# Four chained image layers: u's last steps before z's last product, zero products at the start, and a written order for the last half

## The chip, the cores and the metric

The kernel runs on one core of one Trainium2 chip. The metric is the device time of one execution in microseconds. Besides, one execution was taken with the hardware profiler, and every line of a profile below comes from that execution.

## The reference

The input x has 8 images of 512 channels and 32 x 32 = 1024 pixels, in float32. Four layers follow one another, each on the whole of the one before:

```python
# layer 0: products of two normed projections, scaled by their largest singular value
f, g = relu(batchnorm(Wf @ x)), relu(batchnorm(Wg @ x));  h = Wh @ x      # 64 x 1024 per image
z = f.T @ g;  x = Wv @ (z / sigma_max(z) @ h.T).T + x
# layer 1: group norm, attention of 1024 pixels over 512 channels
n = group_norm(x);  x = x + Wp @ (softmax(q(n).T @ k(n) / sqrt(512)) @ v(n))
# layer 2: attention with 128 channels, then a projection z back to 512
x = bn(Z @ (softmax(t.T @ p / sqrt(128)) @ g)) + x
# layer 3: binary 512 x 512 product
y = (sign(W) * mean|W|) @ sign(x + bias);  t = bn(y) + x - shift
out = where(t > 0, t, slope * t) + bias2
```

The change touches the places where layer 2 ends and layer 3 begins for each image, where layer 1 of the next image starts, the very start, and the very end.

## The kernel before, in words

**Stages.** In the first some 180 us all images go through layer 0's projections (loop over `b`, `products` at L1380 to L1389: 64 x 512 products of weights `fg` and `h` with x). For image 0 the loop runs over the four blocks `cc` of 128 channels and does both f and g for a block before it takes the next. The x tile of an image is loaded by `load_x` (L136) on SP's queue, one transfer per channel block, the first block of image 0 in two halves; the weights `fg` come over ScalarE's queue, one transfer per block. After the statistics, singular values and folded weights are made, `fast` (L919) is called for one image after another, eight times. In it TensorE's program is the order in which the Python text draws it (`manual_schedule` for PE); the order of the other engines' instructions is set by a planner, which goes by its own estimate of when each is ready. An instruction marked with `keep_in_program_order` stays where the text has it. On every engine the instructions then run in that fixed order.

**Two-by-two products with seven multiplications.** Large products are cut into 2 x 2 blocks and done with seven block products, `seven` (L350). Its steps are, in order: A11B11, S1T1, S2T2, S4B22, S3T3, A12B21, A22T4. Each is drawn by one `next`. S1T1, S2T2 and so on are products of sums of blocks. A11B11, S2T2, S3T3 and A22T4 accumulate in one PSUM bank, S1T1 and S4B22 in another; after each step the bank is read by ScalarE (`move`, L358 or L360) or added to the result by VectorE (`plus`, L364 or L366). So A22T4 may only start when the addition after S3T3 has read the bank. The matmuls of all these products have line L413. One product of 128 x 128 weights by 512 pixels in float32 shows as two records 0.43 us apart.

**u.** `make_u` (L498) makes u = wu n for the *next* image, in two groups of seven steps. Behind the last step VectorE makes the block sums of u (`sums_of`, L326): S1 (L331), S2 (L334), S3 in place (L335) and S4 (L336), which the scores of the next image need. The steps are a generator, `steps`, and `fill(k)` draws k of them, as work with which TensorE covers waits.

**The end of layer 2 and layer 3.** `close2` (L705) multiplies z's weights by the attention result of one half (512 pixels): four products (L709), each added to x by VectorE (L711). `leave` (L713) is layer 3 for a half: ScalarE takes the signs of the four channel blocks (L720), TensorE multiplies them by the packed signs of the weights in float16 (L732), ScalarE and VectorE unpack (L743 to L745), scale and add x (L753), and form the two-sided slope: relu (L775), scale (L776), sum (L783), store (L787). For the images with a successor the second half of `leave` stops after the signs, is put into `rest3`, and is taken up by the next call of `fast`: after the first and after the third step of its scores (`scores1`) one `next` is drawn, and each begins with a sign product.

The order of the text before, per image with a successor, is then: the first half of layer 3; `close2` of the second half; the signs of the second half; two more steps of u by `fill(2)`; the rest of u; the next image's scores.

**The last image.** Its layer 3 uses unpacked signs, one product per 128 output channels (L732, `signs`). The first half and the first pair of products of the second take VectorE's maximum (L759), ScalarE's scale (L762) and GpSimd's sum (L769); the last pair goes by relu, scale and VectorE's sum (L775, L776, L783), the very last in two halves of 256. `count_bad` (L801) counts values out of bounds with one small product (L823), casts it (L824) and loads the number into a register of every engine (L825), since a branch (L1778) at the end decides on it whether a slower path runs. In the order of the text this load stands behind the first product of the second half.

Of the kernel before, what the change touches and what calls it, by code (L numbers as in the profile page):

```python
# [16 lines left out]
P = 128  # L17
# [70 lines left out]
def kernel(  # L88
# [55 lines left out]
    def half(i):  # L144
        return bass.ts(i, HF)
# [8 lines left out]
    def load_w(name, src, shape, pool=wpool, eng=nc.sync, tag=None):  # L154
        t = pool.tile(shape, F32, tag=tag or name, name=name)
        eng.dma_start(out=t, in_=src)
        sbw[name] = t
        return t
# [6 lines left out]
    for cc in range(CC):  # L165
        nc.scalar.dma_start(out=fg[:, cc, :], in_=w_fg[:, cc, :])
    first = load_x(0, True)
    load_w("h", w_h, [P, CC, MID], a1, nc.scalar)


# [64 lines left out]
    def col(name, i):  # L235
        return ct[:, COL[name] + i : COL[name] + i + 1]
# [476 lines left out]
    def leave(env, xt, dst, halves=range(NH), signs=None, stop=False):  # L713


        small = env["small"]
        for h in halves:
            sg = env["e"].tile([P, CC, HF], F16, tag="e", name="sg")
            for cc in range(CC):
                nc.scalar.activation(  # L720
                    sg[:, cc, :], xt[:, cc, half(h)], AF.Sign, bias=rb3[:, cc : cc + 1]
                )
            if stop:
                yield
            for j in range(CC // 2):
                both = env["e"].tile([P, 2, HF], F32, tag="e", name="both")
                y1, y2 = both[:, 0, :], both[:, 1, :]

                def product(lt):
                    ps = bank()  # L730
                    for cc in range(CC):
                        mm(  # L732
                            out=ps,
                            lhsT=lt[:, cc, bass.ts(j, P)],
                            rhs=sg[:, cc, :],
                            start=cc == 0,
                            stop=cc == CC - 1,
                        )
                    return ps

                if signs is None:
                    ps = product(sw3)
                    nc.scalar.activation(y2, ps, AF.Identity, bias=round3, scale=1.0 / PACK)  # L743
                    nc.vector.tensor_scalar(y2, y2, ROUND, None, ALU.subtract)
                    nc.vector.scalar_tensor_tensor(y1, y2, -PACK, ps, ALU.mult, ALU.add)  # L745
                    sums = y1, y2
                else:
                    sums = [product(signs[0])]
                    yield
                    sums.append(product(signs[1]))  # L750

                for y, ps, oc in ((y1, sums[0], j), (y2, sums[1], j + 2)):
                    nc.vector.scalar_tensor_tensor(  # L753
                        y, ps, sa3[:, oc : oc + 1], xt[:, oc, half(h)], ALU.mult, ALU.add
                    )
                    up = small.tile([P, HF], F32, tag="half_a", name="up3")
                    if signs is not None and (h == 0 or j == 0):

                        nc.vector.tensor_scalar(  # L759
                            up, y, nc3[:, oc : oc + 1], ps3[:, oc : oc + 1], ALU.max, ALU.mult  # L760
                        )
                        nc.scalar.activation(  # L762
                            y,
                            y,
                            AF.Identity,
                            bias=qb3[:, oc : oc + 1],
                            scale=col("L3_conv_pr_slope", oc),
                        )
                        nc.gpsimd.tensor_tensor(y, y, up, ALU.add)  # L769
                        nc.sync.dma_start(out=dst[:, oc, half(h)], in_=y)  # L770
                        continue
                    final = signs is not None and y is y2
                    for q in (slice(0, HF // 2), slice(HF // 2, HF)) if final else [slice(0, HF)]:
                        yq, uq = y[:, q], up[:, q]
                        nc.scalar.activation(uq, yq, AF.Relu, bias=cb3[:, oc : oc + 1])  # L775
                        nc.scalar.activation(  # L776
                            yq,
                            yq,
                            AF.Identity,
                            bias=pb3[:, oc : oc + 1],  # L780
                            scale=col("L3_conv_pr_slope", oc),
                        )
                        nc.vector.scalar_tensor_tensor(  # L783
                            yq, uq, ps3[:, oc : oc + 1], yq, ALU.mult, ALU.add
                        )
                        to = slice(h * HF + q.start, h * HF + q.stop)
                        nc.sync.dma_start(out=dst[:, oc, to], in_=yq)  # L787
                yield

    def unpacked(env):  # L790

# [127 lines left out]
    def fast(env, n, hb, ua):  # L919
# [90 lines left out]
        if more:  # L1010
            r = inverse_sums(env, esum, B + n)
            values2(0, range(2, NTH))
            att = values2(0, range(NTH, NT))
            values2(1, range(0, NTH))
            close2(xt, att, 0)
            att = values2(1, range(NTH, NT))
            fill()
            for i, _ in enumerate(leave(env, xt, dst, [0])):
                fill(2 * (i % 2))
            close2(xt, att, 1)  # L1020
            rest3.append(leave(env, xt, dst, [1], stop=True))
            next(rest3[0])
            fill(2)
            for _ in steps:
                pass
        else:


            r = inverse_rows(env, esum, B + n)
            att = values2(0, range(2, NT))  # L1030
            values2(1, range(0, 2))
            close2(xt, att, 0)
            values2(1, range(2, 6))
            before, after = leave(env, xt, dst, [0], signs), leave(env, xt, dst, [1], signs)
            count = count_bad(env)
            next(count)
            next(before)
            next(before)
            att = values2(1, range(6, NT))
            next(before)  # L1040
            close2(xt, att, 1)
            for _ in before:
                pass
            next(after)
            next(count)
            for _ in after:
                pass
# [322 lines left out]
    for b in range(B):  # L1370
        xt = load_x(b) if b else first
        for name, src, pool in later.get(b, ()):
            load_w(name, src, shapes.get(name, [P, CC, C]), pool)
        if b in (2, 3, 4, 5):
            load_blocks(*((("q", w_q), ("k", w_k))[b // 2 - 1]), ((0, 1), (2, 3))[b % 2])
        if b >= B - 2:
            resident[b] = xt
        banks = [bank() for _ in w0[: 3 if b < B - 2 else 2]]

        def products(i, cc):  # L1380
            for h in range(NH):
                mm(
                    out=banks[i][side(h), :],
                    lhsT=w0[i][:, cc, :],
                    rhs=xt[:, cc, half(h)],
                    start=cc == 0,
                    stop=cc == CC - 1,
                )

        if b == 0:  # L1390
            for cc in range(CC):
                for i in range(2):
                    products(i, cc)
        for i in range(3):
            if i == 2 and b >= B - 2:
                continue
            if b or i == 2:
                for cc in range(CC):
                    products(i, cc)
            if i == 0:  # L1400
                nc.scalar.copy(fs[b], banks[i])
                nc.vector.bn_stats(st[:, 0, b, :], fs[b])
            elif i == 1:
                nc.vector.tensor_copy(gs[b], banks[i])
                nc.vector.bn_stats(st[:, 1, b, :], gs[b])
                if last is not None:
                    turn(last[0], last[1], ht_pair[last[0] // 2], 0)
        if b < B - 2:
            hraw = a2.tile([P, HF], F32, tag="hraw", name="hraw")
            nc.scalar.activation(hraw, banks[2], AF.Identity, bias=bhc)  # L1410
            last = b, hraw
        else:
            last = None
        if b == 3:
            total3 = sign_weights()
        if b == 5:
            scale_signs(total3)
        if b > 5:
            natural(*((("q", "w3"), ("k", "q"))[b - 6]))
# [415 lines left out]
```

## Time and profile before

| | us |
|---|---|
| median of 3 runs (1883.66 to 1883.94) | 1883.89 |
| the profiled execution | 1883.68 |
| its span, first to last instruction | 1881.8 |
| TensorE busy in the span | 1854.7 |
| VectorE, ScalarE, GpSimd busy | 1124.5, 540.8, 121.8 |
| mean granted TensorE clock | 0.998 |

The profile's page gives busy times, the costliest groups of instructions and the chain that ended last; further views list who waited for whom, and the instructions of one engine in order of time. In a line of the timeline the first number is the start in us from the beginning of the span, the second the time from there to the end of the last of the instructions merged in the line; then come the engine, the line in the code, the operation, `output<-inputs`, and at the end how many. In brackets stands how long the engine had been idle, and who released it. Letters: PE is TensorE's matmul, PEld its weight load, DVE VectorE, ACT ScalarE, POOL GpSimd, SP the queue of most transfers. In a list of waits the numbers are the total in us, how often, and the longest. Names of tiles: `bank` is a PSUM bank, `ut` is u, `us` its block sums, `h` and `hs` the normed image and its block sums, `wu` and `su` the weights of u and their sums, `att` the attention result, `z` z's weights, `xt` the image, `sg` its signs, `sw` and `signs` the packed and unpacked signs of layer 3's weights, `both` and `up` the working tiles of layer 3.

### The profile page before, as it was taken

Reading aid. Unit: us, or ns where it says so; the run is one execution under the profiler, and the core shown is the slowest. Engines: PE = TensorE matmul, PEld = TensorE weight load, DVE = VectorE, ACT = ScalarE, POOL = GpSimd, SP = SyncE. Lnnn points to the kernel's source line nnn. Section 1 sums busy time; section 2 is a strip of 40 time slices with the busy share of each in tenths; the row PEclk is TensorE's granted clock in tenths of the full one; section 3 lists DMA queues with packets and bytes.
Section 4 is the critical chain, followed back from the end, with each engine's and each line's share of the span. In section 5 each row is a group of like instructions: output and inputs, shape, how many; then the busy total and the mean of one; then the engine's idle time right before and its main releaser. Section 6 shows DMA issues by size and latency. Waiting matters only on the chain. (4 is left out here: it accounts for less than half of the span.)

```text
span 1881.8 us, 16542 instructions
## 1 busy us (share of the span) xinstructions
PE 1854.7 (99%) x6196; PEld 948.8 (50%) x6196; DVE 1124.5 (60%) x2083; ACT 540.8 (29%) x882; POOL 121.8 (6%) x109
## 2 busy tenths in 40 slices
PE   8999999999999999999999999999999999999997
PEld 4365464544644464544645465544644464544653
DVE  3356777466744767566754676356633766355447
ACT  2042220343113521244202521244203521243113
POOL 1000002000010001100020001100110001000011
PEclk9999999999999999999999999999999999999999
DMA  8620000002000200002000200002000200000001
GB/s 280 200 85 7 1 17 1 1 34 73 12 1 12 90 17 1 1 34 73 12 1 12 90 18 0 1 34 67 12 0 12 90 12 0 1 34 23 12 0 47
DMA packets 32738, 66.52 MB, mean 35 GB/s; under 512 B 4944, under 2 KB 12300, under 8 KB 32524
## 3 DMA queue, kind: packets, MB, share of 16 engines
q1 hardware_dynamic: 31724, 64.96, 10.4%
q8 instruction: 51, 0.84, 0.2%
q10 hardware_dynamic: 864, 0.43, 0.1%
q14 instruction: 35, 0.29, 0.1%
q0 software_dynamic: 64, 0.00, 0.0%
HBM read 46.44 MB, written 18.94 MB: 35 GB/s over the span
## 5 line engine op out<-in xcount | busy, mean ns | idle before, releaser
L591 PE MATMUL bank<-e,vt 128*128 128x512 f32 x768 | 336.2, 594 | 0.0
L591 PEld LDWEIGHTS bank<-e,vt 128*128 128x128 f32 x768 | 144.3, 190 | 172.3 <-issue 167.9
L413 PE MATMUL bank<-ut,h 128*128 128x512 f32 x384 | 178.5, 599 | 0.2
L413 PEld LDWEIGHTS bank<-ut,h 128*128 128x128 f32 x384 | 70.7, 190 | 97.4 <-issue 91.3
L413 PE MATMUL bank<-us,hs 128*128 128x512 f32 x256 | 115.6, 593 | 0.0
L840 PE MATMUL bank<-tpg 128*128 128x512 f32 x256 | 115.4, 595 | 0.0
L993 PE MATMUL bank<-e,tpg 128*128 128x512 f32 x256 | 114.7, 595 | 0.0
L364 DVE TENSOR_TENSOR e<-bank,e 128x512 f32<-128x512 f32 x96 | 66.2, 689 | 62.9 <-PE bank L413 57.5
L847 ACT ACTIVATE e<-bank 128x512 f32<-128x512 f32 x128 | 76.3, 597 | 67.0 <-PE bank L840 67.0
L358 ACT COPY e<-bank 128x512 f32<-128x512 f32 x96 | 56.0, 583 | 123.4 <-PE bank L413 123.4
L413 PE MATMUL bank<-wo,h 128*128 128x256 f32 x384 | 89.8, 384 | 0.0
L413 PE MATMUL bank<-h,wu 128*128 128x512 f32 x192 | 89.0, 594 | 0.8 <-DVE h L488 0.8
L244 POOL TENSOR_TENSOR r_r<-r_v,minus_half 128x4 f32<-128x4 f32 (+1 forms) x11 | 10.8, 987 | 1050.5 <-DVE r_v L243 1045.2
L993 PEld LDWEIGHTS bank<-e,tpg 128*128 128x128 f32 x256 | 48.1, 190 | 60.4 <-issue 60.0
L413 PEld LDWEIGHTS bank<-wo,h 128*128 128x128 f32 x384 | 71.4, 190 | 12.6 <-issue 3.8
L413 PEld LDWEIGHTS bank<-us,hs 128*128 128x128 f32 x256 | 48.4, 190 | 57.5 <-issue 56.2
L852 DVE TENSOR_TENSOR esum<-esum,e 128x1024 f32<-128x1024 f32 x48 | 58.8, 1226 | 30.1 <-ACT e L847 29.9
L840 PEld LDWEIGHTS bank<-tpg 128*128 128x128 f32 x256 | 47.6, 190 | 55.0 <-issue 52.4
L720 ACT ACTIVATE sg<-xt,rb 128x512 f16<-128x512 f32 x64 | 44.2, 716 | 107.3 <-DVE xt L711 104.4
L364 DVE TENSOR_TENSOR vt<-bank,vt 128x512 f32<-128x512 f32 x48 | 33.2, 692 | 66.4 <-PE bank L413 65.6
L358 ACT COPY vt<-bank 128x512 f32<-128x512 f32 x64 | 37.4, 584 | 121.3 <-PE bank L413 121.2
L358 ACT COPY ut<-bank 128x512 f32<-128x512 f32 x48 | 28.1, 586 | 127.9 <-PE bank L413 127.9
(361 smaller groups left out, 2914.4 us busy)
## 6 DMA issues: line engine op xcount, KB each, us to landing
xt<-in_x SPq DMA_DIRECT2D x55, 512.0 KB
out<-both SPq DMA_DIRECT2D x63, 256.0 KB
rfull<-r_dram SPq DMA_DIRECT2D x15, 512.0 KB
f_dram<-f SPq DMA_DIRECT2D x8, 256.0 KB
fb<-f_dram SPq DMA_DIRECT2D x8, 256.0 KB
w<-in_w SPq DMA_DIRECT2D x1, 1024.0 KB
blocks_q<-in_w_q SPq DMA_DIRECT2D x16, 64.0 KB
blocks_k<-in_w_k SPq DMA_DIRECT2D x16, 64.0 KB
```

The costliest lines, as they stand in the source:

```text
L244: nc.gpsimd.tensor_tensor(r, v, minus_half[:, 0:n], ALU.pow)
L358: nc.scalar.copy(dst, ps)
L364: nc.vector.tensor_tensor(dst, ps, u, ALU.add)
L413: mm(out=ps[:, q * w : (q + 1) * w], lhsT=lt(ka, kb, q, k), rhs=rhs(ka, kb, q, k), start=first and q == 0 and k == 0, stop=last and k == 1 ...
L591: mm(out=ps, lhsT=a[:, t, bass.ts(r_, P)], rhs=e[t], start=first and t == 0, stop=last and t == NTH - 1, skip_group_check=True,)
L720: nc.scalar.activation(sg[:, cc, :], xt[:, cc, half(h)], AF.Sign, bias=rb3[:, cc : cc + 1])
L840: mm(out=ps, lhsT=pt[:, 0, bass.ts(t, P)], rhs=tt[:, 0, half(h)], start=True, stop=True,)
L847: nc.scalar.activation(e[:, half(h)], ps, AF.Exp, scale=float(P) ** -0.5)
L852: nc.vector.tensor_tensor(esum, esum, e, ALU.add)
L993: mm(out=banks[h], lhsT=gt[:, t, :], rhs=es[t][:, half(h)], start=t == 0, stop=t == NT - 1,)
```

## The change

Four things are edited. (1) At the start a tile `still` of 128 x 128 zeros is set by VectorE and multiplied by itself seven times, ahead of all other products; the first real product is pinned behind that. (2) In `fast`, for images with a successor, all remaining steps of u are drawn ahead of `close2` of the second half instead of behind it. (3) The second half of layer 3 of the last image gets a function of its own, `last_half`, with the order of ScalarE's and VectorE's instructions pinned: the first of its four results ends on GpSimd as before, the second by relu, scale and VectorE, the third and fourth by maximum, a scale into a tile of its own (`scaled`), and a sum on VectorE, the fourth in two halves. It yields once more, right after the signs, so that the load of the count stands ahead of its first product. (4) In `leave` the branches that only served that half are taken out.

```diff
@@ start
     first = load_x(0, True)
+    still = a1.tile([P, P], F32, tag="still", name="still")
+    nc.vector.memset(still, 0.0)
+    ps = bank()
+    for _ in range(7):
+        nc.tensor.matmul(out=ps[:, 0:P], lhsT=still, rhs=still, start=True, stop=True)
     load_w("h", w_h, [P, CC, MID], a1, nc.scalar)
@@ leave
-                    if signs is not None and (h == 0 or j == 0):
+                    if signs is not None:
...
+    def last_half(env, xt, dst, signs):
+        h = 1
+        keep = tc.keep_in_program_order
...
+        yield
+        names = ("both", "both", "up3", "scaled")
+        a, b, ups, zs = (env["e"].tile([P, 2, HF], F32, tag="e", name=name) for name in names)
...
+        form(0)
+        above(0)
+        scaled(0, ys[0], qb3)
+        nc.gpsimd.tensor_tensor(ys[0], ys[0], up[0], ALU.add)
+        store(0)
+        form(1)
+        keep(nc.scalar.activation(up[1], ys[1], AF.Relu, bias=cb3[:, 2:3]))
+        scaled(1, ys[1], pb3)
+        form(2)
+        form(3)
+        scaled(2, zs[:, 0], qb3)
+        above(2)
+        keep(nc.vector.scalar_tensor_tensor(ys[1], up[1], ps3[:, 2:3], ys[1], ALU.mult, ALU.add))
+        store(1)
+        above(3)
+        keep(nc.vector.tensor_tensor(ys[2], zs[:, 0], up[2], ALU.add))
+        store(2)
+        for q in (slice(0, HF // 2), slice(HF // 2, HF)):
+            scaled(3, zs[:, 1], qb3, q)
+            keep(nc.vector.tensor_tensor(ys[3][:, q], zs[:, 1, q], up[3][:, q], ALU.add))
+            store(3, q)
+        yield
@@ fast, an image with a successor
             for i, _ in enumerate(leave(env, xt, dst, [0])):
                 fill(2 * (i % 2))
+            for _ in steps:
+                pass
             close2(xt, att, 1)
             rest3.append(leave(env, xt, dst, [1], stop=True))
             next(rest3[0])
-            fill(2)
-            for _ in steps:
-                pass
@@ fast, the last image
-            before, after = leave(env, xt, dst, [0], signs), leave(env, xt, dst, [1], signs)
+            before, after = leave(env, xt, dst, [0], signs), last_half(env, xt, dst, signs)
@@ products of layer 0
-                mm(
+                one = mm(
...
+                if b + i + cc + h == 0:
+                    tc.keep_in_program_order(one)
```

In `last_half`, `form(n)` is the product of the signs for one block of 128 output channels and the sum with x on VectorE (as L753), `above(n)` is VectorE's maximum (as L759), `scaled(n, ...)` is ScalarE's scale (as L762 or L776), and `store(n)` is the transfer to the output.

More of the change, by code (lines that the diff above doesn't have):

```diff
@@ L771, in leave @@
                         continue
[L772 to L787, printed above, removed]
@@ L788, in leave @@
-                yield
+                    nc.scalar.activation(up, y, AF.Relu, bias=cb3[:, oc : oc + 1])
+                    nc.scalar.activation(
+                        y,
+                        y,
+                        AF.Identity,
+                        bias=pb3[:, oc : oc + 1],
+                        scale=col("L3_conv_pr_slope", oc),
+                    )
+                    nc.vector.scalar_tensor_tensor(
+                        y, up, ps3[:, oc : oc + 1], y, ALU.mult, ALU.add
+                    )
@@ new lines, in leave, with form, above, scaled @@
+                    nc.sync.dma_start(out=dst[:, oc, half(h)], in_=y)
+                yield
+    def last_half(env, xt, dst, signs):
+        h = 1
+        keep = tc.keep_in_program_order
+        sg = env["e"].tile([P, CC, HF], F16, tag="e", name="sg")
+        for cc in range(CC):
+            nc.scalar.activation(
+                sg[:, cc, :], xt[:, cc, half(h)], AF.Sign, bias=rb3[:, cc : cc + 1]
+            )
+        yield
+        names = ("both", "both", "up3", "scaled")
+        a, b, ups, zs = (env["e"].tile([P, 2, HF], F32, tag="e", name=name) for name in names)
+        ys = [a[:, 0], a[:, 1], b[:, 0], b[:, 1]]
+        up = [env["small"].tile([P, HF], F32, tag="half_a", name="up3") for _ in range(2)]
+        up += [ups[:, i] for i in range(2)]
+        def form(n):
+            j, i = n // 2, n % 2
+            oc = j + 2 * i
+            ps = bank()
+            for cc in range(CC):
+                mm(
+                    out=ps,
+                    lhsT=signs[i][:, cc, bass.ts(j, P)],
+                    rhs=sg[:, cc, :],
+                    start=cc == 0,
+                    stop=cc == CC - 1,
+                )
+            keep(
+                nc.vector.scalar_tensor_tensor(
+                    ys[n], ps, sa3[:, oc : oc + 1], xt[:, oc, half(h)], ALU.mult, ALU.add
+                )
+            )
+        def above(n):
+            oc = n // 2 + 2 * (n % 2)
+            keep(
+                nc.vector.tensor_scalar(
+                    up[n], ys[n], nc3[:, oc : oc + 1], ps3[:, oc : oc + 1], ALU.max, ALU.mult
+                )
+            )
+        def scaled(n, z, bias, q=slice(0, HF)):
+            oc = n // 2 + 2 * (n % 2)
+            keep(
+                nc.scalar.activation(
+                    z[:, q],
+                    ys[n][:, q],
+                    AF.Identity,
+                    bias=bias[:, oc : oc + 1],
+                    scale=col("L3_conv_pr_slope", oc),
+                )
+            )
+        def store(n, q=slice(0, HF)):
+            oc = n // 2 + 2 * (n % 2)
+            to = slice(h * HF + q.start, h * HF + q.stop)
+            nc.sync.dma_start(out=dst[:, oc, to], in_=ys[n][:, q])
+        form(0)
[20 more added lines that the diff above has]
+        yield
```

## Prediction

> **What bounds the kernel now.** First the page, part 1: TensorE is the bound, everything else has room.
>
> ```profile
> PE 1854.7 (99%) x6196; PEld 948.8 (50%) x6196; DVE 1124.5 (60%) x2083; ACT 540.8 (29%) x882; POOL 121.8 (6%) x109
> ```
>
> Only what opens or closes a gap on PE, or shifts its first or last work, moves the end. So next PE's list of waits (total us, times, longest):
>
> ```profile
> PE bank L413 <- DVE ut L366: 6.1, 7, 0.9
> PE bank L1382 <- DMA fg<-in_w_fg: 4.8, 1, 4.8
> ```
>
> The first recurs once per image but the last; all seven look alike to 0.02 us. I read one on the timeline, 604 to 642, PE first:
>
> ```profile
> 617.25 1.88 PE L413 MATMUL bank<-h,su 128*128 128x512 f32 x4
> 618.96 3.60 PE L709 MATMUL bank<-att,z 128*128 128x512 f32 x8
> 622.40 3.60 PE L413 MATMUL bank<-h,wu 128*128 128x512 f32 x8
> 626.86 1.98 PE L413 MATMUL bank<-hs,wu 128*128 128x512 f32 x4 [0.87 <-DVE ut L366]
> 628.68 1.88 PE L413 MATMUL bank<-ut,h 128*128 128x512 f32 x4
> 630.40 1.03 PE L732 MATMUL bank<-sg,sw 128*128 128x512 f16 x4
> 631.26 3.60 PE L413 MATMUL bank<-us,hs 128*128 128x512 f32 x8
> ```
>
> z's products (618.96) stand ahead of the last three steps of u. The last of these waits for a DVE addition. Layer 3's sign product (630.40) starts without a wait. DVE, same window, is packed:
>
> ```profile
> 621.69 0.75 DVE L366 SCALAR_TENSOR_TENSOR ut<-bank,bu,ut 128x512 f32<-128x512 f32 x1
> 624.27 1.88 DVE L711 TENSOR_TENSOR xt<-bank,xt 128x512 f32<-128x512 f32 x3
> 626.06 1.40 DVE L366 SCALAR_TENSOR_TENSOR ut<-bank,bu,ut 128x512 f32<-128x512 f32 x2
> 627.38 1.22 DVE L331 TENSOR_TENSOR us<-ut 128x1024 f32<-128x1024 f32 x1
> 628.63 1.23 DVE L334 TENSOR_TENSOR us<-us,ut 128x1024 f32<-128x1024 f32 x1
> 629.77 1.22 DVE L335 TENSOR_TENSOR ut<-ut 128x1024 f32<-128x1024 f32 x1
> ```
>
> All four xt sums precede u's. ScalarE has its four signs by 626.9, 3.5 us before PE needs them:
>
> ```profile
> 624.99 1.95 ACT L720 ACTIVATE sg<-xt,rb 128x512 f16<-128x512 f32 x3 [1.07 <-DVE xt L711]
> ```
>
> Last the two ends:
>
> ```profile
> 4.83 9.31 PE L1382 MATMUL bank<-xt,fg 128*64 128x512 f32 x32 [4.83 <-DMA fg<-in_w_fg]
> 1869.50 2.75 PE L732 MATMUL bank<-sg,signs 128*128 128x512 f16 x12 [0.81 <-DVE bad L824]
> 1871.42 1.47 DVE L759 TENSOR_SCALAR up<-both,nc,ps 128x512 f32<-128x512 f32 x1
> 1876.54 0.98 DVE L783 SCALAR_TENSOR_TENSOR both<-up,ps,both 128x256 f32<-128x256 f32 x2 [0.54 <-ACT both L776]
> ```
>
> **What the Trainium skill says.** "TensorE: Matmul & The Clock Gate", Part 1: the array starts at half clock and goes to full after some 3.4 us of work; as long an idle time takes it back. The trace agrees: weight loads come in pairs 0.85 us apart until 8.0, 0.43 us apart from 8.8. The same page, Part 2: matmuls stay in program order, only weight loads are pulled ahead; so one late operand holds all behind it, as at 626.86. "SBUF — State Buffer", Who interferes with whom: VectorE's tensor_scalar can hold, or wait for, a port pair that GpSimd needs. It agrees: L759 takes 0.55 us alone, 1.47 when begun beside GpSimd's addition.
>
> **The change, part by part**
>
> *1. z's products behind the last steps of u, seven times.* I take each engine's new order from the compiled program. PE: S4B22, S3T3, A12B21, A22T4, four z, A11B11 of the scores, then at once the sign product. DVE: up to 621.69 as before; then two ut additions, two L783, the third ut addition, S1, **one** xt, S2, S3, S4, **three** xt. ACT: the four signs, with one copy (of the scores' A11B11) after the first. Start-to-start steps, from this trace: 0.66 us for an L366 or L783, 1.14 for a sum of 1024, 0.60 for an xt.
>
> PE: S3T3 starts at 618.96, A12B21 ends at 618.96 + 2 x 1.72 = 622.40. A22T4 goes into the bank that the second ut addition reads. That runs 622.35 to 623.09; A22T4 starts at 623.14 (0.75 lost; before, 625.83 to 626.86, 1.03). Gain 0.28. Then 623.14 + 1.82 = 624.97; z's four to 624.97 + 3.43 = 628.40; A11B11 to 630.12. The sign product stands there.
>
> DVE: 623.01 and 623.67 L783, 624.33 ut, 624.99 S1, 626.13 first xt (its product is out at 626.0), 626.74 S2, 627.88 S3, 629.02 S4, then 630.15, 630.76, 631.36 the three xt, the last ending at 632.04. ACT's copy ends near 630.9, so signs start at 630.88, 631.50 and 632.12; the last, of 0.71 us, ends at 632.8. The last of four sign matmuls starts at 632.87 and ends a 0.22 later, 633.1; the restart after a gap costs about 0.1 (0.53 against 0.43 at 626.86), perhaps not all. The next product, S1T1, therefore starts near 633.13 where it was 631.26: **+1.87 us** an image, the 0.28 already in it. So the stall goes from a DVE addition to the signs, and what hid them (3.5 us) is used up by three sums of u that moved in front of three xt. Behind the held product queue the scores' products, for which nobody else has work; after it ACT and DVE follow PE at the old distances (L743, L744), so nothing is won back. SP's stores of this half, and the x loads behind them, go 1.9 us later, with no reader near. 7 x 1.87 = **+13.1 us**.
>
> *2. Seven products of zeros.* One VectorE memset (bounded by 0.3 us, beside DMA waits) from 0.7, then 14 passes. Warm, 32 passes of this size take 3.73 us (L692 at 559.92), so cold 14 x 0.23 = 3.3: 1.0 to 4.3, before the data at 4.83. If this opens the clock, cold work from 4.83 to 8.8 would be 4.0/2 = 2.0 us shorter. But loads then bind: by the trace's landings x's channel blocks 1, 2, 3 are complete at 6.94, 8.81 and 11.52, and block 3's first matmul ran at 11.83. The gain is what lies between: **-0.3** (bounds -2.0, if block 3 came sooner, and +0.5, if the zeros ran a few us long: block 3's landing hides most of that). Pinning the first real product behind them adds nothing.
>
> *3. The last half.* Up to the signs nothing changes; GpSimd loses one addition, and one L759-like step falls behind the next form. The bad-count is now read ahead of form 0: cast near 1868.2, PE restarts about 0.5 us later (as 1868.95 to 1869.50 now), at 1868.86, behind the last sign (1868.15). Four products of 0.86 end at 1872.3 (before 1872.1). DVE's and ACT's own reads of the count move into their streams, beside a wait for form 0 (1869.9): nothing; uncovered, about 0.5. SP's read waits ahead of a store that is ready only at 1871.1: nothing. Then DVE is the chain: above 0 waits out GpSimd's addition to 1871.4; forms 1, 2, 3 from 1871.35, 1872.0, 1872.66 (last product out at 1872.5); above 2 from 1873.3 to 1873.8, behind GpSimd once more; then +0.7 (L862), +0.5 (above 3), +0.65, and two halves of 0.4: end 1876.5 against 1877.51. The stores go through SP at 0.35 us each, the last at 1876.5 against 1877.54, and 384 KB behind one another still clear by then at the rate of the page (some 390 GB/s in the start). **-1.0** (bounds -0.4, -1.4).
>
> *Sum.* Profiled execution 1883.68 = span 1881.8 + 1.9 around it; the median 1883.89 is 0.2 above, within the runs' spread. 1883.68 + 13.1 - 0.3 - 1.0 = **1895.5**.
>
> **Rivals.** *(a) Not slower: the signs come in time.* Place: the sign product after A11B11. Price: without that wait only gains stay, 7 x 0.28 + 0.3 + 1.0 = 3.3, 1880.4. It decides at 630.77 (630.12 + three matmuls of 0.216): the last sign would have to end there, 2.0 us before my 632.8. z's products are out at 628.6, so the data allow it. Against: three sums of 1.14 stand in front, in an in-order engine without a gap. *(b) The clock falls in the seven gaps.* 3.4 us at half rate costs 1.7: 7 x 1.7 = 12 more, 1907.5. For: PE has some 2 us of near-idleness. Against: shorter than the page's window, three small matmuls fall in it, and the granted clock stays at 0.998 with gaps up to 1.1 us. *(c) The start pays in full,* block 3 landing sooner in another execution: 1.7 more, 1893.8. Against: landings don't depend on PE, and the three runs lie within 0.3 us.
>
> **Numbers.** As computed 0.77; (c) 0.12; (a) 0.07; (b) 0.04. The unknowns of the sum (start, tail, +-0.2 per image in part 1) give 1892.5 to 1898.5, which takes in (c); left out are (a), (b) and some 0.07 of misjudged size. A measurement here tells about 0.2%, 3.8 us, from no change. Slower by more 0.92, within 0.05 (most of a), faster 0.03.
>
> **What would show it.** PE's waits: the ut entry shrinks, and seven waits of the sign product for ACT's signs, 2 us each, appear. Timeline: A22T4 0.75 us after A12B21; signs ending 4.4 us after z's last product. Start: paired loads 0.43 us apart from the first, a wait for x near 11.5. End: last DVE work 1.0 us sooner after the last sign. Wrong if the three xt don't follow S4, or the sign product doesn't wait.

## The result, and the profile after

| | before | after |
|---|---|---|
| median, us | 1883.89 (5 runs, 1883.22 to 1884.39) | 1894.26 (5 runs, 1893.97 to 1894.73) |
| the profiled execution, its span | 1883.68, 1881.8 | 1894.27, 1892.3 |
| mean granted TensorE clock | 0.998 | 0.999 |

The changed kernel is slower: ratio 1.0056, 95% interval 1.0041 to 1.0070, a median difference of 10.4 us. The line numbers after stand 5 further down (L413 is L418, L709 is L714, L711 is L716, L720 is L725, L732 is L737). So S1 to S4, L331 to L336 before, are L336, L339, L340 and L341 now: L336 was S4 and is S1. The last half's products are L812, the count's cast is L907.

PE's list of waits in the changed kernel, total us, times, longest:

```profile
PE bank L737 <- ACT sg L725: 11.2, 21, 1.1
PE bank L418 <- DVE ut L371: 4.1, 7, 0.6
```

The wait for u's addition is still there and 2.0 us smaller in all. A new one has come, three times for each of the seven images with a successor: layer 3's sign product (the product of the packed weights with the signs) waits for ScalarE's signs. The timeline of the changed kernel around the same image, PE first (start, us to the last end, engine, line, operation, tiles, how many, idle time before and its releaser):

```profile
623.44 1.98 PE L418 MATMUL bank<-hs,wu 128*128 128x512 f32 x4 [0.58 <-DVE ut L371]
625.26 3.60 PE L714 MATMUL bank<-att,z 128*128 128x512 f32 x8
628.69 1.88 PE L418 MATMUL bank<-ut,h 128*128 128x512 f32 x4
630.41 0.38 PE L737 MATMUL bank<-sg,sw 128*128 128x512 f16 x1
631.91 0.38 PE L737 MATMUL bank<-sg,sw 128*128 128x512 f16 x1 [1.12 <-ACT sg L725]
...
633.35 3.59 PE L418 MATMUL bank<-us,hs 128*128 128x512 f32 x8
```

The first sign matmul runs at 630.41, since one sign is ready; the other three come 0.61 apart behind the signs, and S1T1 begins at 633.35, where without a wait it would have begun at 631.27 (630.41 and four matmuls of 0.216). That is a stall of 2.08 us. VectorE and ScalarE in the same stretch:

```profile
625.28 1.21 DVE L336 TENSOR_TENSOR us<-ut 128x1024 f32<-128x1024 f32 x1
626.42 0.68 DVE L716 TENSOR_TENSOR xt<-bank,xt 128x512 f32<-128x512 f32 x1
627.02 1.21 DVE L339 TENSOR_TENSOR us<-us,ut 128x1024 f32<-128x1024 f32 x1
628.15 1.21 DVE L340 TENSOR_TENSOR ut<-ut 128x1024 f32<-128x1024 f32 x1
629.28 1.22 DVE L341 TENSOR_TENSOR us<-ut,us 128x1024 f32<-128x1024 f32 x1
630.42 1.88 DVE L716 TENSOR_TENSOR xt<-bank,xt 128x512 f32<-128x512 f32 x3
...
630.61 0.58 ACT L363 COPY e<-bank 128x512 f32<-128x512 f32 x1 [2.75 <-PE bank L418]
631.13 1.95 ACT L725 ACTIVATE sg<-xt,rb 128x512 f16<-128x512 f32 x3
```

z's last product was out near 628.9; its sum with x, and two more, stand behind S2, S3 and S4 until 630.42. That is the whole chain of the loss: three sums of u, three sums of x, three signs, the held product.

The two ends of the changed kernel:

```profile
1.06 3.36 PE L172 MATMUL bank<-still 128*128 128x128 f32 x14 [1.06 <-DVE still L169]
4.46 8.45 PE L1464 MATMUL bank<-xt,fg 128*64 128x512 f32 x32
...
1879.84 3.61 PE L812 MATMUL bank<-sg,signs 128*128 128x512 f16 x16 [1.28 <-DVE bad L907]
...
1886.56 0.74 DVE L869 TENSOR_TENSOR both<-scaled,up 128x256 f32<-128x256 f32 x2
```

The 32 records of the first image's f and g take 8.45 us to the last end, where they took 9.31. Their weight loads show how TensorE's pace changes:

```profile
5.11 0.49 PEld L1464 LDWEIGHTS bank<-xt,fg 128*64 128x64 f32 x3 [0.36 <-DMA xt<-in_x]
5.97 0.24 PEld L1464 LDWEIGHTS bank<-xt,fg 128*64 128x64 f32 x2 [0.37 <-issue]
10.97 0.20 PEld L1464 LDWEIGHTS bank<-xt,fg 128*64 128x64 f32 x4 [0.81 <-DMA xt<-in_x]
```

From 5.11 to 5.97 it is 0.86 us, half pace; the next pair comes at 6.40, after 0.43. So the first real products still ran at half pace, for some 1.5 us. At 10.97 TensorE has waited for block 3 of image 0, the last of its four.

**Where the time went.** Each matmul of the changed kernel can be laid beside the same matmul of the kernel before. The shift is -1.25 us behind the start, stays there to 388, falls by 0.23 at image 0's first z product, grows by 1.78 at each of the seven images (2.08 of stall, less the 0.30 by which A22T4 waits shorter), and is +10.99 at the last image's z. From there VectorE's last work gains 1.20, and the span ends only 0.49 sooner than that shift. -1.25 - 0.23 + 7 x 1.78 - 0.49 = 10.5, which is the difference of the spans (1892.31 - 1881.81); the profiled executions differ by 10.6.

### The profile page after: what moved, and what is told of

Read it like the earlier page. It is cut to its first block, busy times and chain, and to the rows that moved or that the text cites. A ratio compares the mean times of both kernels' runs of the same rounds, so it can differ in the third digit from the quotient of the medians.

```text
span 1892.3 us, 16558 instructions
## 1 busy us (share of the span) xinstructions
PE 1860.2 (98%) x6210; PEld 946.6 (50%) x6210; DVE 1123.6 (59%) x2086; ACT 539.9 (29%) x880; POOL 119.9 (6%) x108
## 4 chain that ended last, share of the span: by engine, by line
PE 93%; DVE 5%; ACT 2%; issue 0%; POOL 0%; DVEq 0%; ACTq 0%
PE bank L418 43%; PE bank L596 20%; PE bank L923 6%; PE bank L1076 6%; PE bank L1464 4%; PE bank L697 3%; PE bank L714 3%; PE bank L442 1%; DVE both L758 1%; PE bank L737 1%; ACT sg L725 1%; PE wide L1512 1%; PE bank L1143 1%; PE bank L1570 1%; PE quad L1356 0%; DVE ut L371 0%
## 5 line engine op out<-in xcount | busy, mean ns | idle before, releaser
L418 PE MATMUL bank<-ut,h 128*128 128x512 f32 x384 | 178.5, 599 | 0.2
L418 PEld LDWEIGHTS bank<-ut,h 128*128 128x128 f32 x384 | 70.7, 190 | 97.3 <-issue 91.3
L418 PE MATMUL bank<-us,hs 128*128 128x512 f32 x256 | 115.6, 593 | 0.0
L418 PE MATMUL bank<-wo,h 128*128 128x256 f32 x384 | 89.9, 384 | 0.0
L418 PE MATMUL bank<-h,wu 128*128 128x512 f32 x192 | 89.0, 594 | 0.7 <-DVE h L493 0.7
L418 PEld LDWEIGHTS bank<-us,hs 128*128 128x128 f32 x256 | 48.4, 190 | 60.3 <-issue 59.8
L418 PEld LDWEIGHTS bank<-wo,h 128*128 128x128 f32 x384 | 71.4, 190 | 12.6 <-issue 3.8
L725 ACT ACTIVATE sg<-xt,rb 128x512 f16<-128x512 f32 x60 | 41.8, 718 | 106.5 <-DVE xt L716 103.6
```

What stands on the lines that cost most here:

```text
L418: mm(out=ps[:, q * w : (q + 1) * w], lhsT=lt(ka, kb, q, k), rhs=rhs(ka, kb, q, k), start=first and q == 0 and k == 0, stop=last and k == 1 ...
L725: nc.scalar.activation(sg[:, cc, :], xt[:, cc, half(h)], AF.Sign, bias=rb3[:, cc : cc + 1])
```

## The experiments

The theory was the prediction's: VectorE's order makes the stall, since three sums of u came in front of three sums of xt. Rivals: the loss lies in the ends; or TensorE's order makes it, because behind z's products only A11B11 is left as cover. All nine kernels compute the whole reference. They ran on three chips, whose medians of the kernel before were 1883.88 (the first four below), 1883.32 (the next four) and 1883.55 (the last); each is set against the one of its own chip. Where a run is compared with the changed kernel, that is its 1894.26, measured beside 1883.89 for the kernel before.

**The move alone**, on the kernel before:

```diff
+            for _ in steps:
+                pass
             close2(xt, att, 1)
             rest3.append(leave(env, xt, dst, [1], stop=True))
             next(rest3[0])
-            fill(2)
-            for _ in steps:
-                pass
```

> Only the move of u's last steps ahead of z's products, nothing else of the change. Theory (seven stalls of the sign product, each because three sums of u stand in front of three sums of xt on VectorE): 7 x 1.79 = 12.5 us over the kernel before, 1896.4. Rival (the lost time is in the two ends or in the clock, and the move by itself is neutral or a gain of 7 x 0.28): 1882 to 1884.

1896.14 us, 12.3 over before, ratio 1.0067 (1.0053 to 1.0081). In its trace PE's wait for the signs is again 11.2 us in 21 parts, and the shift grows by 1.79 at each of the seven images. The move is the loss, and more than the whole of it.

**The changed kernel without the move**: the same lines, the other way round.

> The changed kernel with the move undone: zeros and the written last half stay. Theory: 12.5 us under the changed kernel, near 1881.8, that is 2.0 under the kernel before (start 1.48, tail 0.55). Rival (the start's 1.48 was a matter of when the blocks of x happened to land in one execution): 1883.0. If the parts work on one another, neither: the sum of the parts would miss by more than 0.5.

1882.15 us, 1.7 under before, ratio 0.9991 (0.9983 to 1.0000). With the run above, 12.3 - 1.7 = 10.5: within the runs' spread the parts add up to the change's 10.4, and nothing shows that they work on one another. The theory's 2.0 and the rival's 0.9 lie on both sides of 1.7; further runs below take the two ends apart.

**u's sums behind z's sums, TensorE's order untouched.** In the changed kernel, `done` of u's second group, which makes the block sums, is held back until the signs are drawn:

```diff
+        def ended():
+            if held:
+                held[:] = [done]
+            else:
+                done()
...
-                then=done if i else None,
+                then=ended if i else None,
...
+            held.clear()
+            held.append(None)
             for _ in steps:
                 pass
             close2(xt, att, 1)
             rest3.append(leave(env, xt, dst, [1], stop=True))
             next(rest3[0])
+            held.pop()()
```

> The changed kernel with TensorE's order untouched; only VectorE's block sums of u are drawn behind z's additions to xt, so that they come in the order S1, two xt, S2, two xt, S3, S4. Theory (VectorE's order makes the stall): the signs end some 0.1 to 0.5 us ahead of or behind their product, the seven stalls of 1.1 to 2 us go or nearly go, and only the gain of 0.28 an image stays: 1879.8 to 1881.5. Rival (TensorE's order makes it: behind z's products only A11B11 is left as cover, too little for addition, signs and products whatever VectorE does first): 1890 or more.

1877.97 us, ratio 0.9971 (0.9959 to 0.9982): 5.9 under before and 16.3 under the changed kernel. Its timeline at the same image (lines of layer 3 stand 6 further down than in the changed kernel, so the sums of xt are L722, the signs L731, the sign product L743):

```profile
628.43 1.03 PE L743 MATMUL bank<-sg,sw 128*128 128x512 f16 x4
...
624.43 1.45 DVE L722 TENSOR_TENSOR xt<-bank,xt 128x512 f32<-128x512 f32 x2
625.80 1.22 DVE L339 TENSOR_TENSOR us<-us,ut 128x1024 f32<-128x1024 f32 x1
626.93 1.28 DVE L722 TENSOR_TENSOR xt<-bank,xt 128x512 f32<-128x512 f32 x2
628.13 1.22 DVE L340 TENSOR_TENSOR ut<-ut 128x1024 f32<-128x1024 f32 x1
...
627.65 1.33 ACT L731 ACTIVATE sg<-xt,rb 128x512 f16<-128x512 f32 x2 [1.01 <-DVE xt L722]
```

The sums of xt end at 628.21 and the signs at 628.98; the four sign matmuls, 0.216 apart from 628.43 on, need the last sign at 629.08. They run without a gap. TensorE's 6210 recorded matmuls come in the same order as in the changed kernel, one for one. So A11B11 alone is cover enough, and TensorE's order by itself doesn't make the stall: the rival has fallen. With one order of VectorE the same matmuls lose 2.08 us an image, with the other nothing. Not all of the 16.3 is that stall, 7 x 2.08 = 14.6: ScalarE's order has changed too, and the last experiment below shows that this was worth some 2 us.

**u's last step behind z's products.** In the changed kernel, two of the three last steps are drawn ahead:

```diff
-            for _ in steps:
-                pass
+            fill(2)
             close2(xt, att, 1)
             rest3.append(leave(env, xt, dst, [1], stop=True))
             next(rest3[0])
+            for _ in steps:
+                pass
```

> The changed kernel, but only two of the three last steps of u stand ahead of z's four products; the last step (A22T4) and with it all block sums of u stand behind them. Theory: z's products cover the wait of A22T4 for the second addition to u, and A22T4 and A11B11 cover the signs, since no sum of u is ahead of a sum of xt any more: both stalls go, 7 x (1.79 + 1.03) = 19.7 under the changed kernel, 1874.5. Rival (the stall moves again: the block sums of u, now begun later, hold up S1T1 of the scores or layer 3's unpacking): 1877 to 1884, with a new wait in PE's list behind the sign product.

1872.22 us, ratio 0.9942 (0.9928 to 0.9955): 11.7 under before, 22.0 under the changed kernel. Its timeline:

```profile
620.03 3.60 PE L714 MATMUL bank<-att,z 128*128 128x512 f32 x8
623.47 1.88 PE L418 MATMUL bank<-hs,wu 128*128 128x512 f32 x4
625.18 1.88 PE L418 MATMUL bank<-ut,h 128*128 128x512 f32 x4
626.90 1.03 PE L737 MATMUL bank<-sg,sw 128*128 128x512 f16 x4
```

A22T4 no longer waits for the addition, which now runs beside z's four products, and the signs have A22T4 and A11B11 as cover. Both entries are gone from PE's list of waits. But this version and the one before it were 2.3 and 1.8 us better than the theory's sums (the second figure counts from the lower end of its range), so something was missing in them; the last experiment asks what.

**The zeros alone**, on the kernel before.

```diff
     first = load_x(0, True)
+    still = a1.tile([P, P], F32, tag="still", name="still")
+    nc.vector.memset(still, 0.0)
+    ps = bank()
+    for _ in range(7):
+        nc.tensor.matmul(out=ps[:, 0:P], lhsT=still, rhs=still, start=True, stop=True)
...
+                if b + i + cc + h == 0:
+                    tc.keep_in_program_order(one)
```

> The kernel before with the seven products of zeros and the pinned first product alone. Theory (the array is at full clock from the first real product, then the landings of x's blocks bind): 0.6 to 1.3 us off, 1882.9, with the waits for x longer than before. Rival 1 (the clock counts in full, the loads hide nothing): 2.0 off, 1881.9. Rival 2 (the 0.9 to 1.25 us that four executions with the zeros gained in the start were only earlier landings, as one execution without zeros gained 0.73): 1883.9.

1882.67 us against 1883.32, medians of 13 and 33 runs: 0.65 less, but the ratio's interval, 0.9988 to 1.0005, holds no change too. The traces help: the last of the first image's 32 records of f and g is followed by h's products at 13.69, 12.96, 13.90 and 13.11 in four executions without the zeros, and at 12.74, 13.09, 12.89, 12.75, 12.84 and 12.51 in six with seven of them, means 13.4 and 12.8. These times also hold when x landed, and that varies: block 3 was whole between 10.38 and 11.52 in the eleven profiled executions. Free of it is the time from that landing to the first matmul that needed the block: 0.32, 0.47, 1.57 and 0.72 us without zeros, 0.04 in six of the seven executions with zeros and 0.18 in the other. So the gain isn't one of earlier landings only, and rival 2 has fallen. The full 2.0 us of rival 1 didn't come: PE waits 1.01 us for x's last block in this run, which it reaches early now. The theory fell in one point, for the array was not at full pace from the first real product (4.71) but from 6.06.

**Fourteen products of zeros** (`range(14)` in the same place).

> The same with fourteen products of zeros instead of seven, so that they end some 1.5 us later, near 6.0, and the first real product with them. Theory (landings bind behind it): within 0.3 us of the run with seven, the waits for x shorter by what the zeros took. Rival (TensorE's own work binds there): 1.5 us slower than with seven.

1883.00 us, ratio 0.9998 (0.9989 to 1.0006), 0.33 over the run with seven. The first real product ran at 6.00 instead of 4.71, now at full pace from the start, yet PE still waited 0.98 us for the last block of x: the landings bind, the 1.5 us of the rival are excluded, and a warmer array gained nothing more.

**The written last half alone**, on the kernel before (`last_half`, the added yield and `leave` as in the change, the rest left out).

> The kernel before with the written last half alone. Theory: VectorE's last work ends 1.2 us sooner after the last signs, but the last stores land 0.7 to 0.8 later after their issue (2.7 against 1.9 us): 0.55 off, 1883.3. Rival (the late landings were one execution's): 1.2 off, 1882.7.

1882.92 us against 1883.32, ratio 0.9998 (0.9990 to 1.0006): 0.4 less, which the times can't tell from none. The trace repeats the changed kernel's: the last three stores are whole 3.18, 3.08 and 2.81 us after their issue (changed kernel 3.05, 2.97 and 2.69; kernel before 2.01, 1.92 and 1.89). So the late landings belong to this tail, not to one execution: in all six profiled executions with the written half the last store is whole 2.69 to 2.83 us after its issue, in the five without it 1.84 to 2.00. The two ends apart, 0.65 and 0.4, make less than the 1.7 that they made together on another chip; with intervals of some 1.5 us to each side that is no contradiction, and no proof of the sum.

**The last three stores from ScalarE**, in the version with u's last step behind z's products:

```diff
+        def store(n, q=slice(0, HF), by=nc.sync):
...
-        store(2)
-        for q in (slice(0, HF // 2), slice(HF // 2, HF)):
-            scaled(3, zs[:, 1], qb3, q)
+        halves = slice(0, HF // 2), slice(HF // 2, HF)
+        for q in halves:
+            scaled(3, zs[:, 1], qb3, q)
+        store(2, by=nc.scalar)
+        for q in halves:
             keep(nc.vector.tensor_tensor(ys[3][:, q], zs[:, 1, q], up[3][:, q], ALU.add))
-            store(3, q)
+            store(3, q, nc.scalar)
```

> The version with u's last step behind z's products, with the last three stores issued by ScalarE, behind its last scale, instead of SP. In the written last half two of the sixteen parts of each of the last three stores land 1.1 us behind the others (3.1 against 2.0 us after the issue). Theory A (SP's queue makes it: its stores stand behind one another): all parts land some 2.0 us after issue, the end comes 0.7 to 0.9 sooner, 1871.4. Theory B (the two DMA engines are busy with something else at that time, whatever queue a store comes from): the last three stores land 2.7 to 3.1 us after their issue as before, 1872.2.

1871.87 us, ratio 0.9938 (0.9925 to 0.9952), not told apart from the same version with SP's stores. The three stores are whole 3.15, 3.00 and 2.83 us after their issue, again with one or two of their sixteen parts 0.2 to 1.1 us behind the others. Theory A has fallen. The Trainium skill, "DMA: Bandwidth & Descriptors", Issuing engines are not separate DMA queues, says that transfers started by the scalar, sync or gpsimd engine end up on the same 16 DMA engines. The run fits that, since the late parts come from either queue. What holds them up was not tried.

**One copy by VectorE**, on the kernel before, off the change:

```diff
-        move(c12, va, None)
+        if aside:
+            nc.vector.tensor_copy(c12, va)
+        else:
+            move(c12, va, None)
...
-                term, lo[:, half(0)], hi[:, half(0)], lo[:, half(1)], hi[:, half(1)], exp=scale
+                term, lo[:, half(0)], hi[:, half(0)], lo[:, half(1)], hi[:, half(1)], exp=scale, aside=bool(rest3)
```

> The kernel before with one edit, off the change: for the first group of an image's scores the bank of S1T1 and S2T2 is copied by VectorE instead of ScalarE, where the copy stands behind four instructions of layer 3 until 636.86 although the product was out at 634.9. It asks why two versions were 1.8 to 2.3 us better than their sum. Theory (the list of waits leaves out a stall of S3T3: it starts 1.91 us after the product ahead of it, not 1.72, and its second half 0.53 later, not 0.43, because it may only write the bank when that copy has read it): 7 x 0.29 = 2.0 us off, 1.72 and 0.43 in the trace. Rival (the 0.29 is the product's own, or VectorE's copy of 0.6 us brings another wait): within 0.5 us of the kernel before, or slower.

1881.21 us against 1883.55, ratio 0.9988 (0.9982 to 0.9995), 2.3 less. The copy is the one after S2T2, and its bank is the one of A11B11 and S2T2, to which S3T3 adds. The kernel before, S4B22 and S3T3 of the scores and ScalarE:

```profile
635.56 1.88 PE L413 MATMUL bank<-us,h 128*128 128x512 f32 x4
637.47 3.70 PE L413 MATMUL bank<-ut,h 128*128 128x512 f32 x8
...
636.86 0.56 ACT L358 COPY e<-bank 128x512 f32<-128x512 f32 x1
```

and with the copy on VectorE:

```profile
634.65 1.88 PE L416 MATMUL bank<-us,h 128*128 128x512 f32 x4
636.37 3.60 PE L416 MATMUL bank<-ut,h 128*128 128x512 f32 x8
...
633.99 0.69 DVE L383 COPY e<-bank 128x512 f32<-128x512 f32 x1
```

From one product to the next it is 1.91 us before and 1.72 now, and the x8 line 3.70 long before and 3.60 now. Together 0.30 us an image, at each of the seven. Before, the copy ends at 637.42 and S3T3 starts at 637.47; with the copy done by 634.68 nothing holds it. This stall stands in no list of waits: the ends of matmuls are modelled, and by them S3T3 follows without idle time. In the changed kernel it is still there (1.91 and 3.70 at 639.55). In the two faster versions the planner, given another order, put the copy ahead of layer 3's activations (at 631.40 in the version with the last step behind), so the stall went without being aimed at: 7 x 0.30 = 2.1 us, the missing part.

## Why the prediction was right, and where its sizes were off

**z's products behind the last steps of u: right in mechanism and close in size.** The changed kernel lies 0.30 us later than the kernel before at this image, so that much comes off its starts. A22T4 at 623.14 (predicted 623.14), A11B11 at 628.39 (628.40), the first xt at 626.12 (626.13), the three late ones from 630.12 (630.15), the end of the signs at 632.78 (632.8), S1T1 at 633.05 (633.13). The last step is the only one that differs: the restart after the gap, put at about 0.1 us with a "perhaps not all", cost almost nothing behind a matmul that had waited. So 1.78 instead of 1.87 an image and 12.5 instead of 13.1 for the seven. That the stall goes "from a DVE addition to the signs" is shown by the wait list, and that VectorE's order makes it by the version with the sums behind, which leaves TensorE's order as it is.

**The start: mis-sized.** The term was -0.3; the changed execution gained 1.25 there, and the zeros alone some 0.65 by medians and by the mean of executions. That the loads bind is what the traces show. A warm array from the first real product, "paired loads 0.43 us apart from the first", is not: full pace began at 5.97 in the changed kernel, and between 5.3 and 6.7 in the six executions with seven zeros. With fourteen it was there, and the gain was no larger. The term itself was one execution's gap between a landing and a matmul (11.52 and 11.83), the smallest of the four without zeros, whose largest is 1.57. And landings are not that fixed: block 3 was complete at 11.52 before and at 10.92 after, though nothing of the change touches its load. So of the 1.25 some 0.3 is the gap (0.32 before, 0.04 after), which closed as predicted, and 0.6 is an earlier landing, which was luck; the other 0.37 comes behind that matmul and was not followed. Rival (c) argued with landings that don't depend on PE; true, but they vary by more than the term from execution to execution.

**The last half: half the gain.** Up to VectorE's last work the steps held: relative to the last image's z, the cast came at 1868.16 (predicted 1868.2), PE again at 1868.85 (1868.86), the last addition's end at 1876.31 (1876.5, before 1877.51). What failed is "384 KB behind one another still clear by then": the last store landed whole 2.69 us after its issue instead of 1.89. The 390 GB/s behind that step are a rate of loads in the start (395 between 6 and 8 us), not of stores. Of 0.96 us gained at the store's issue, 0.80 went there; 0.33 came back between that landing and the end. That stretch is 2.05 us in all six executions with the written half and 2.29 to 2.43 in the five without; why was not followed. So -0.49 instead of -1.0, inside the bounds of -0.4 and -1.4.

**Not in the sum:** 0.23 us at image 0's first z product, once. It isn't the move's: that product starts 0.43 us after the one ahead of it in the changed kernel and in the move alone, but also in the last half alone, and 0.58 to 0.83 after it in the other eight. Why it varies was not followed.

**The rivals.** (a) fell, since the sign product waits; the reordering shows the condition that it needed, the sums of xt ahead of those of u. (b) fell: the granted clock stayed at 0.999 through seven stalls of about 2 us, and the records behind them stand 0.43 us apart as before. (c) is half true, as above. The predicted 1895.5 against 1894.26 is the sum of -0.6 in the seven images, -0.95 in the start, -0.23 at image 0 and +0.5 in the tail.

## What to carry to other kernels

Moving a product earlier can move its consumers too: before TensorE's order is changed, write down the order that VectorE and ScalarE then get. Here VectorE got three sums that TensorE didn't need yet in front of three that it did wait for, and ran them in that order. Put as much work behind the urgent product as covers its chain of reads: one step of u more behind z was the difference between 10 us lost and 12 won, of which some 2 came from the copy's place and not from the step. A wait that no list names can be found by start-to-start distances of products that should be alike.

## What the runs showed of the hardware

- Products of zeros open TensorE's clock. Among the 28 passes of zeros the starts are 0.213 us apart up to 4.4 us and 0.112 from then on, 3.4 us after the first. The Trainium skill, "TensorE: Matmul & The Clock Gate", Part 1, gives some 3.4 us of sustained work for this; this run agrees, and shows that zeros count as work. It isn't a fixed time: with 14 passes of zeros and then real products full pace came 4.3 to 5.6 us after the first pass (six executions), without zeros 3.4 to 5.2 us after the first product (four).
- In the written last half one or two of the sixteen parts of each of the last three stores land up to 1.2 us behind the rest, 2.7 to 3.2 us after issue, from SP's queue (five executions) and from ScalarE's (one). The other fourteen land at 1.7 to 2.1. In the five executions without it the last three stores are whole after 1.8 to 2.1.
